# Expert blocks of two sizes, and 8 KB reads and 4 KB writes in the last stage of a Mamba, SSD and experts kernel

## The chip, the cores and the metric

The kernel runs on one core of a Trainium2 chip, in one launch. The metric is the device time of that launch in microseconds. Engines are named as in the profile: PE (matmuls; PEld its weight loads), DVE (vector), ACT (scalar), POOL (GpSimd) and SP, which here only issues DMAs.

## The reference

The input x has 4 images of 256 channels and 64 x 64 points, so 16,384 tokens of 256 channels, all in float32. Layer 0 is a gated Mamba block, layer 1 a Mamba-2 (SSD) block. After them comes a mixture of eight experts, which sends each token to the one expert with the largest gate value. Each expert takes at most 2,560 tokens (1.25 x 16384 / 8). The part that matters here, shortened:

```python
idx = jnp.argmax(probs, axis=-1)                    # one expert for a token
pos = (jnp.cumsum(one_hot, axis=0) * one_hot).sum(-1).astype(jnp.int32) - 1
buf = jnp.zeros((E, C, D), dtype=h.dtype).at[idx, pos_safe].set(x, mode='drop')
hmid = jax.nn.relu(jnp.einsum('ecd,edf->ecf', buf, w1) + b1[:, None, :])
ybuf = jnp.einsum('ecf,efd->ecd', hmid, w2) + b2[:, None, :]
y_tok = ybuf[idx, pos_g] * (prb * kept)[:, None]
```

Here E = 8, C = 2560, D = 256 and F = 1024. At the end the tokens (token by channel) are turned back into images (channel by point).

## The kernel before, in words

The program has three phases, called one after the other at the end of `tile_conv_attn_hybrid`: `mixers`, `experts` and `turn`.

**mixers** computes both layers in 64 chunks of 256 tokens. Its instructions are not issued as written: they are collected in a `Plan`, which orders them by a simulated schedule with costs and due slots, and `issue` emits them in that order (so nearly all of them have line 373 in the profile). For each token it writes the layer's output to `tok_d` in DRAM, and scatters a row of 260 numbers (probability, scale, shift, token number, 256 channels) to `buf_d`, at the slot that the token has in its expert's part of 2,560 slots.

The end of `mixers`, from line 1270, makes the tables that the experts read. `total` holds each expert's number of tokens. A block is 256 slots of one expert. From the counts the code works out how many blocks each expert needs (`blocks`), the running sum of them (`ends`), and for each of 71 blocks which expert it belongs to (`which`) and where its rows begin (`base`). The results are `row_at` (two columns of row numbers for each block) and `w_at` (the rows of the expert's weights). 71 is NT // st + NE - 1, with st = 256: enough for any routing. All 71 blocks are always run; a block without tokens reads row numbers that are out of use. The table's operations are small ones on DVE, each needing the one before it. They work in the space of three tiles of the `mid` ring, handed out by `line`.

**experts** runs over the 71 blocks. `begin(i)` (line 1351) gathers the block's rows (`rows`, two indirect DMAs of 128 rows, on POOL) and the weights of its expert (`w`, one indirect DMA of 128 x 17,440 bytes), normalises the tokens on ACT (`tn`, line 1362), converts the token numbers on DVE (`number`, line 1364) and turns the tokens on PE (`pt`, line 1369), which DVE copies to `xt` (line 1370). Then, for eight slices `f` of the hidden layer, PE computes `ph` (line 1387) with the weights as the stationary operand and the 256 tokens as the moving one; ACT makes `hid` of six slices (line 1389) and DVE of two (line 1391). In the middle of these slices `begin(i + 1)` is called. Then PE computes `po` (line 1398) for each half of 128 tokens, with `hid` as the stationary operand and 256 columns of `w2` as the moving one. DVE and ACT make the result `fixed` from it (lines 1399 to 1408), and POOL scatters it to `tok_d` with one indirect DMA for each half (line 1410). There are three buffers for `w`, four for `rows` and `number`, two for the other work tiles, and in PSUM four for `ph` and two each for `pt` and `po`. In this phase the framework's own scheduler orders the instructions of each engine when the program is built; an engine then runs them in that fixed order.

**turn** reads `tok_d` in 32 pieces of 512 tokens (`outrows`, issued by SP, line 1429), so that partition p has tokens p, p + 128, p + 256 and p + 384: pieces of 1 KB. PE turns them into `pto` (line 1434), DVE and ACT copy a channel half each to `o` (lines 1436 and 1438), and ACT issues the write (line 1439): 2 KB for a channel. There are six buffers for `outrows`, `o` and `pto`.

Of the kernel before, what the change touches and what calls it, by code (L numbers as in the profile page):

```python
# [20 lines left out]
P = 128  # L21
# [362 lines left out]
def tile_conv_attn_hybrid(ctx: ExitStack, tc: tile.TileContext, a: dict, out: bass.AP, cap: int, st: int):  # L384
# [12 lines left out]
    def nm(s):  # L397
        return f"{s}_{next(names)}"
# [9 lines left out]
    ident = const.tile([P, P], F32, name="ident")  # L408
    make_identity(nc, ident)

    nj = st // P
    nblk = NT // st + NE - 1
    row_at = const.tile([P, nblk, nj], U32, name="row_at")
    w_at = const.tile([P, nblk], U32, name="w_at")

    def column(value):
        t = const.tile([P, 1], F32, name=nm("col"), tag=nm("col"))
# [8 lines left out]
    def mixers(es):  # L426
# [214 lines left out]
        for t in (s_in, s_out, s_cb, s_cbbc, s_dtb, neg_a1, g_b, taps_x, diag_bc, diag_d1):  # L641
            t.root.lasting = True

        routed, rows_at, ws_at = r.fixed(buf_d), r.fixed(row_at), r.fixed(w_at)

        def load_x(k_, tag):
            xin = work([P, KC, T], tag)
# [639 lines left out]
        def iota(t, step, n, cm=0):  # L1287
            r.gps("iota", t, [[step, n]], 0, cm, allow_small_or_imprecise_dtypes=True)
            return t
# [2 lines left out]

            return t[:, :, None].to_broadcast([P, *n]) if inner else t[:, None].to_broadcast([P, *n])

        per = cap // st
        steps, block, which_e = iota(line(0, per), st, per), iota(line(0, nblk), 1, nblk), iota(line(0, NE), 1, NE)
        place = iota(line(0, nj), P, nj, 1)
        counts, one, blocks, ends, starts = (line(0, NE) for _ in range(5))
        which, count, base, limit = (line(0, nblk) for _ in range(4))
        some = line(0, NE, per)  # L1300
        r.gps("memset", one, 1.0)
        r.copy(counts, total)
        r.tt(some, over(counts, (NE, per), True), over(steps, (NE, per), False), ALU.is_gt)
        r.dve("tensor_reduce", blocks, some, AX.X, ALU.add)
        r.dve("tensor_tensor_scan", ends, one, blocks, 0.0, ALU.mult, ALU.add)
        r.tt(starts, ends, blocks, ALU.subtract)
        n = (nblk, NE)
        table = line(1, *n)
        r.tt(table, over(block, n, True), over(ends, n, False), ALU.is_ge)
        r.dve("tensor_reduce", which, table, AX.X, ALU.add)  # L1310
        mine = line(2, *n)
        r.tt(mine, over(which, n, True), over(which_e, n, False), ALU.is_equal)
        for sums, values in ((base, starts), (count, counts)):
            r.tt(table, mine, over(values, n, False), ALU.mult)
            r.dve("tensor_reduce", sums, table, AX.X, ALU.add)

        r.tt(base, block, base, ALU.subtract)
        r.dve("tensor_scalar", base, base, float(st), None, ALU.mult)
        r.dve("scalar_tensor_tensor", count, count, float(cap), base, ALU.min, ALU.subtract)
        r.dve("scalar_tensor_tensor", base, which, float(cap), base, ALU.mult, ALU.add)  # L1320
        r.dve("tensor_scalar", base, base, float(NSLOT), None, ALU.subtract)
        n = (nblk, nj)
        row, valid = line(2, *n), line(2, *n)
        r.tt(valid, over(count, n, True), over(place, n, False), ALU.is_gt)
        r.tt(row, over(base, n, True), over(place, n, False), ALU.add)
        r.tt(row, row, valid, ALU.mult)
        r.dve("tensor_scalar", rows_at, row, float(NSLOT), None, ALU.add)
        r.dve("tensor_scalar", which, which, float(NE - 1), float(P), ALU.min, ALU.mult)
        r.tt(ws_at, which, place[:, :1].to_broadcast([P, nblk]), ALU.add)
        r.issue()  # L1330

    def experts(es):
# [17 lines left out]

        W1, W2 = KC * FF, KF * C

        def begin(i):

            w = wp.tile([P, W1 + W2 + KF + C], F32, name=nm("w"), tag="w")
            rows = wk.tile([P, nj, ROW], F32, name=nm("rows"), tag="rows", bufs=4)
            for j in range(nj):
                gather(rows[:, j], buf_d, row_at[:, i, j : j + 1], NSLOT + P)
            gather(w, a["w_exp"], w_at[:, i : i + 1], NE * P)
            tn = wk.tile([P, nj, C], F32, name=nm("tn"), tag="tn")  # L1360
            for j in range(nj):
                act(tn[:, j], rows[:, j, TOK:], AF.Identity, scale=rows[:, j, 1:2], bias=rows[:, j, 2:3])  # L1362
            number = wk.tile([P, nj], U32, name=nm("number"), tag="number", bufs=4)
            nc.vector.tensor_copy(number, rows[:, :, 3])  # L1364
            xt = wk.tile([P, KC, st], F32, name=nm("xt"), tag="xt")
            pt = pt_p.tile([P, KC, st], F32, name=nm("pt"), tag="pt")
            for k in range(KC):
                for j in range(nj):
                    nc.tensor.transpose(pt[:, k, j * P : (j + 1) * P], tn[:, j, k * P : (k + 1) * P], ident)
            nc.vector.tensor_copy(xt, pt)  # L1370
            return w, rows, number, xt

        now = begin(0)
        for i in range(nblk):
            w, rows, number, xt = now
            w1 = w[:, :W1].rearrange("p (k f) -> p k f", k=KC)
            w2 = w[:, W1 : W1 + W2].rearrange("p (k d) -> p k d", k=KF)
            b1 = w[:, W1 + W2 : W1 + W2 + KF]
            b2 = w[:, W1 + W2 + KF :]
            hid = wk.tile([P, KF, st], F32, name=nm("hid"), tag="hid")  # L1380
            for f in range(KF):
                if f == KF // 2 and i + 1 < nblk:

                    now = begin(i + 1)
                ph = ph_p.tile([P, st], F32, name=nm("ph"), tag="ph")
                for k in range(KC):
                    mm(ph, w1[:, k, f * P : (f + 1) * P], xt[:, k], start=k == 0, stop=k == KC - 1)  # L1387
                if f % 4 != 3:
                    act(hid[:, f], ph, AF.Relu, bias=b1[:, f : f + 1])  # L1389
                else:  # L1390
                    ts(hid[:, f], ph, b1[:, f : f + 1], 0.0, ALU.add, ALU.max)
            y = wk.tile([P, nj, C], F32, name=nm("y"), tag="y")
            fixed = wk.tile([P, nj, C], F32, name=nm("fixed"), tag="fixed")
            ok = wk.tile([P, nj, C], U32, name=nm("ok"), tag="ok", bufs=1)
            po = po_p.tile([P, nj, C], F32, name=nm("po"), tag="po")
            for j in range(nj):
                for f in range(KF):
                    mm(po[:, j], hid[:, f, j * P : (j + 1) * P], w2[:, f], start=f == 0, stop=f == KF - 1)  # L1398
            tt(y, po, b2[:, None].to_broadcast([P, nj, C]), ALU.add)
            for j in range(nj):  # L1400
                act(y[:, j], y[:, j], AF.Copy, scale=rows[:, j, 0:1])

            ts(fixed, y, -1e4, 1e4, ALU.max, ALU.min)
            ts(ok, y, 0.0, 0.0, ALU.mult, ALU.is_equal)
            nc.vector.copy_predicated(fixed, ok, y)
            tt(ok, y, y, ALU.not_equal)
            nc.vector.copy_predicated(fixed, ok, zero[:, None].to_broadcast([P, nj, C]))
            tt(fixed, fixed, rows[:, :, TOK:], ALU.add)  # L1408
            for j in range(nj):
                nc.gpsimd.indirect_dma_start(  # L1410
                    out=tok_d,
                    out_offset=bass.IndirectOffsetOnAxis(ap=number[:, j : j + 1], axis=0),
                    in_=fixed[:, j],
                    in_offset=None,
                    bounds_check=NT - 1,
                    oob_is_err=False,
                )

    def turn(es):

        wk = es.enter_context(tc.tile_pool(name="out_work", bufs=6))
        pt_p = es.enter_context(tc.tile_pool(name="out_ps", bufs=6, space=PSUM))
        W = 512
        nj = W // P
        for b in range(NB):
            for c in range(L // W):
                i = b * L + c * W
                rows = wk.tile([P, nj, C], F32, name=nm("outrows"), tag="outrows")
                nc.sync.dma_start(rows, tok_d[i : i + W].rearrange("(j p) d -> p j d", p=P))  # L1429
                o = wk.tile([P, KC, W], F32, name=nm("o"), tag="o")  # L1430
                for k in range(KC):
                    pt = pt_p.tile([P, W], F32, name=nm("pto"), tag="pto")
                    for j in range(nj):
                        nc.tensor.transpose(pt[:, j * P : (j + 1) * P], rows[:, j, k * P : (k + 1) * P], ident)  # L1434
                    if k % 2 == 0:
                        nc.vector.tensor_copy(o[:, k], pt)  # L1436
                    else:
                        nc.scalar.copy(o[:, k], pt)  # L1438
                nc.scalar.dma_start(out[b].rearrange("(k p) l -> p k l", p=P)[:, :, c * W : (c + 1) * W], o)  # L1439

    for phase in (mixers, experts, turn):
# [101 lines left out]
```

## Time and profile before

| what | us |
|---|---|
| time, median of 3 runs | 6741.11 (6736.48 to 6754.15) |
| the profiled execution's own time | 6746.82 |
| its span, first to last instruction | 6745.1 |
| granted clock of PE, mean over the span | 0.957 of full |
| mixers, until the counts are copied | to 5603.0 |
| table on DVE | 5603.2 to 5611.5 |
| first `ph` matmul, end of the last `po` | 5624.0, 6643.2 |
| first read of the last stage | 6653.7 |

The profile's page gives each engine's busy time, then the span in 40 equal slices (a digit is the busy share in tenths), then DMA queues, then groups of instructions. In a group or a timeline row, `ph<-xt,w` names what is written and what is read, `x16` is the number of instructions, and the part in square brackets is how long the engine had been idle before and what ended this. In a group's line the busy time in us and the mean of one in ns follow the bar, then the idle time before the group's instructions. A float32 matmul appears as two passes. Times in a timeline count from the start of the span.

### The profile page before, as it was taken

Reading aid. Unit: us, or ns where it says so; the run is one execution under the profiler, and the core shown is the slowest. Engines: PE = TensorE matmul, PEld = TensorE weight load, DVE = VectorE, ACT = ScalarE, POOL = GpSimd, SP = SyncE. Lnnn points to the kernel's source line nnn. Section 1 sums busy time; section 2 is a strip of 40 time slices with the busy share of each in tenths; the row PEclk is TensorE's granted clock in tenths of the full one; section 3 lists DMA queues with packets and bytes.
Section 4 is the critical chain, followed back from the end, with each engine's and each line's share of the span. In section 5 each row is a group of like instructions: output and inputs, shape, how many; then the busy total and the mean of one; then the engine's idle time right before and its main releaser. Section 6 shows DMA issues by size and latency. Waiting matters only on the chain. (4 is left out here: it accounts for less than half of the span.)

```text
span 6745.1 us, 111880 instructions
## 1 busy us (share of the span) xinstructions
PE 6239.9 (93%) x37672; PEld 4330.6 (64%) x37672; DVE 5559.2 (82%) x7646; ACT 4878.5 (72%) x12007; POOL 3305.5 (49%) x2632
## 2 busy tenths in 40 slices
PE   7899999999999999999999999999999978999996
PEld 5566666666666666666666666666666546888886
DVE  5999999999999999999999999999999973344443
ACT  6888888888878888888888888888888852333332
POOL 4655555555555555555555555555555542333331
PEclk8999999999999999999999999999999988999998
DMA  6855555555555555555555555555555534555556
GB/s 189 233 151 149 151 149 151 149 147 151 152 148 153 149 148 152 152 153 152 149 150 151 151 153 147 156 151 151 153 149 150 148 92 158 186 196 190 193 191 243
DMA packets 943874, 1077.19 MB, mean 160 GB/s; under 512 B 94480, under 2 KB 912404, under 8 KB 934082
## 3 DMA queue, kind: packets, MB, share of 16 engines
q1 hardware_dynamic: 904594, 842.28, 45.0%
q0 software_dynamic: 30000, 210.98, 8.7%
q10 hardware_dynamic: 8704, 16.78, 0.6%
q8 instruction: 297, 4.87, 0.3%
q14 instruction: 279, 2.29, 0.1%
HBM read 785.70 MB, written 277.68 MB: 158 GB/s over the span
## 5 line engine op out<-in xcount | busy, mean ns | idle before, releaser
L373 POOL TENSOR_TENSOR p<-h,bc 128x1024 f32<-128x1024 f32 x1024 | 2413.7, 2357 | 1996.7 <-DVE ub L373 501.3
L373 DVE TENSOR_TENSOR_SCAN h<-da,ub 128x1024 f32<-128x1024 f32 x1024 | 2339.1, 2284 | 77.0 <-ACT da L373 4.4
L373 ACT ACTIVATE da<-dt,w_m_Alog 128x255 f32<-128x255 f32 x4096 | 1842.7, 502 | 0.0
L373 DVE TENSOR_TENSOR ub<-u,bc 128x1024 f32<-128x1024 f32 x1024 | 1279.1, 1249 | 13.9 <-DMA u<-u_d 6.5
L373 PE MATMUL py<-p,sum 128*32 128x256 f32 x8192 | 658.9, 394 | 175.1 <-POOL p L373 168.8
L373 PE MATMUL b<-t,w_W_in 128*128 128x256 f32 x2304 | 579.0, 392 | 25.2 <-ACT bcs L373 4.8
L373 PEld LDWEIGHTS b<-t,w_W_in 128*128 128x128 f32 x2304 | 418.4, 190 | 188.7 <-ACT raw L373 75.3
L1387 PE MATMUL ph<-xt,w 128*128 128x256 f32 x2272 | 516.3, 381 | 4.0 <-ACT hid L1389 3.9
L373 PE MATMUL a<-t,w_m_in_w 128*128 128x256 f32 x2048 | 513.4, 395 | 3.0 <-DVE t L373 2.7
L1398 PE MATMUL po<-w,hid 128*128 128x256 f32 x2272 | 502.0, 379 | 0.0
L373 PEld LDWEIGHTS py<-p,sum 128*32 128x32 f32 x8192 | 169.0, 108 | 497.3 <-POOL p L373 246.5
L373 PE MATMUL a<-raw,taps_m 128*128 128x256 f32 x2048 | 482.0, 383 | 4.9 <-ACT pre L373 4.9
L1398 PEld LDWEIGHTS po<-w,hid 128*128 128x128 f32 x2272 | 431.7, 190 | 58.7
L1387 PEld LDWEIGHTS ph<-xt,w 128*128 128x128 f32 x2272 | 427.0, 191 | 62.2 <-ACT hid L1389 5.7
L373 PEld LDWEIGHTS a<-t,w_m_in_w 128*128 128x128 f32 x2048 | 372.8, 191 | 145.6 <-issue 72.5
L373 PEld LDWEIGHTS a<-raw,taps_m 128*128 128x128 f32 x2048 | 378.2, 190 | 130.4 <-ACT e L373 39.8
L373 ACT COPY hlast<-h 128x4 f32<-128x4 f32 x1024 | 202.9, 198 | 273.6 <-DVE h L373 260.9
L1364 DVE CAST number<-rows 128x2 uint32<-128x2 f32 x71 | 12.0, 169 | 467.0 <-DMA tok_d<-fixed,number 455.5
L1362 ACT ACTIVATE tn<-rows 128x256 f32<-128x256 f32 x142 | 82.3, 597 | 402.9 <-DMA rows<-buf_d,row_at 397.2
L373 PE MATMUL c<-cum,after 128*128 128x512 f32 x512 | 323.8, 719 | 15.9 <-ACT dend L373 13.5
L1410 POOL DMA_INDIRECT tok_d<-fixed,number x142 | 146.1, 1029 | 391.2 <-DVE fixed L1408 308.5
L373 ACT ACT_TABLE_LOAD x256 | 328.4, 1283 | 4.5
(237 smaller groups left out, 11320.5 us busy)
## 6 DMA issues: line engine op xcount, KB each, us to landing
dt<-dt_d SPq DMA_DIRECT2D x1024, 128.0 KB, 2.8
u<-u_d SPq DMA_DIRECT2D x1024, 128.0 KB, 2.2
raw<-raw_d SPq DMA_DIRECT2D x1024, 128.0 KB, 3.6
gx_d<-pre SPq DMA_DIRECT2D x64, 1024.0 KB, 5.5
bc<-bc_d SPq DMA_DIRECT2D x1024, 64.0 KB, 2.4
gx<-gx_d SPq DMA_DIRECT2D x256, 256.0 KB, 4.8
raw_d<-raw SPq DMA_DIRECT2D x64, 518.0 KB, 3.6
dt_d<-mid SPq DMA_DIRECT2D x64, 512.0 KB
```

The lines of the kernel that those rows point to most:

```text
L373: op.issued = f(*map(placed, args), **{k: placed(v) for k, v in kw.items()})
L1362: act(tn[:, j], rows[:, j, TOK:], AF.Identity, scale=rows[:, j, 1:2], bias=rows[:, j, 2:3])
L1364: nc.vector.tensor_copy(number, rows[:, :, 3])
L1387: mm(ph, w1[:, k, f * P : (f + 1) * P], xt[:, k], start=k == 0, stop=k == KC - 1)
L1398: mm(po[:, j], hid[:, f, j * P : (j + 1) * P], w2[:, f], start=f == 0, stop=f == KF - 1)
L1410: nc.gpsimd.indirect_dma_start(out=tok_d, out_offset=bass.IndirectOffsetOnAxis(ap=number[:, j : j + 1], axis=0), in_=fixed[:, j], in_offse ...
```

## The change

Three things change, and nothing else does.

1. **Blocks of two sizes.** With 128 rows as a unit, 16384 / 128 + 7 = 135 units are enough for any routing. They become 63 blocks of 256 rows and 9 of 128, and each size has tables of its own. The code gives each expert as many big blocks as it has full use for (`pairs`: a second unit must hold tokens), in order of the experts, until 63 are given (`taken`); what is left of each expert (`rest`) goes to small blocks, which begin behind its big ones (`gone`). `line_up` spreads the small blocks evenly among the big ones.
2. **Tables.** What was done once for 71 blocks is done twice, for 63 and for 9, with a few operations ahead of it.
3. **The last stage** takes 1,024 tokens in a piece: partition p reads tokens 8p to 8p + 7, 8 KB in one run. The turned tokens are put in their order by the copy from PSUM, which writes a number to every eighth place (32 bytes apart). A write has 4 KB for a channel. DVE copies one half of the tokens in each partition, ACT the other. There are four buffers in place of six for `outrows` and `o`.

The diff, cut to its core:

```diff
-    nblk = NT // st + NE - 1
-    row_at = const.tile([P, nblk, nj], U32, name="row_at")
-    w_at = const.tile([P, nblk], U32, name="w_at")
+    units = NT // P + NE - 1
+    n_big = (units - NE) // 2
+    sizes = (nj, n_big), (1, units - nj * n_big)
+    tables = [
+        (const.tile([P, n, k], U32, name=f"row_at{k}"), const.tile([P, n], U32, name=f"w_at{k}")) for k, n in sizes
+    ]
...
+        for sums, first, step, n in ((n_units, 0, P, per), (pairs, P, 2 * P, per // 2)):
+            steps, some = line(0, n), line(0, NE, n)
+            r.gps("iota", steps, [[step, n]], first, 0, allow_small_or_imprecise_dtypes=True)
+            r.tt(some, over(counts, (NE, n), True), over(steps, (NE, n), False), ALU.is_gt)
+            r.dve("tensor_reduce", sums, some, AX.X, ALU.add)
+
+        def upto_here(ends, starts, n):
+            r.dve("tensor_tensor_scan", ends, one, n, 0.0, ALU.mult, ALU.add)
+            r.tt(starts, ends, n, ALU.subtract)
+
+        upto_here(ends, starts, pairs)
+        r.dve("tensor_scalar", taken, starts, -1.0, float(n_big), ALU.mult, ALU.add)
+        r.dve("scalar_tensor_tensor", taken, taken, 0.0, pairs, ALU.max, ALU.min)
+        r.dve("scalar_tensor_tensor", rest, taken, -2.0, n_units, ALU.mult, ALU.add)
+        r.dve("tensor_scalar", gone, taken, float(st), None, ALU.mult)
+        for (k, nblk), (rows_at, ws_at), n_blocks, behind in zip(sizes, tables, (taken, rest), (zero_e, gone)):
+            rows_at, ws_at = r.fixed(rows_at), r.fixed(ws_at)
+            upto_here(ends, starts, n_blocks)
+            r.dve("scalar_tensor_tensor", starts, starts, float(-k * P), behind, ALU.mult, ALU.add)
...
-        def begin(i):
+        def begin(nj, i):
             w = wp.tile([P, W1 + W2 + KF + C], F32, name=nm("w"), tag="w")
-            rows = wk.tile([P, nj, ROW], F32, name=nm("rows"), tag="rows", bufs=4)
+            row_at, w_at = tables[nj == 1]
+            st = nj * P
+            rows = wk.tile([P, 2, ROW], F32, name=nm("rows"), tag="rows", bufs=4)[:, :nj]
...
-        now = begin(0)
-        for i in range(nblk):
+        line_up = sorted(((i + 0.5) / n, k, i) for k, n in sizes for i in range(n))
+        now = begin(*line_up[0][1:])
+        for at, (_, nj, _) in enumerate(line_up):
+            st = nj * P
...
-        wk = es.enter_context(tc.tile_pool(name="out_work", bufs=6))
+        wk = es.enter_context(tc.tile_pool(name="out_work", bufs=4))
...
-        W = 512
+        W = 1024
         nj = W // P
+        half = nj // 2
...
-                nc.sync.dma_start(rows, tok_d[i : i + W].rearrange("(j p) d -> p j d", p=P))
+                nc.sync.dma_start(rows, tok_d[i : i + W].rearrange("(p j) d -> p j d", p=P))
                 o = wk.tile([P, KC, W], F32, name=nm("o"), tag="o")
                 for k in range(KC):
-                    pt = pt_p.tile([P, W], F32, name=nm("pto"), tag="pto")
-                    for j in range(nj):
-                        nc.tensor.transpose(pt[:, j * P : (j + 1) * P], rows[:, j, k * P : (k + 1) * P], ident)
-                    if k % 2 == 0:
-                        nc.vector.tensor_copy(o[:, k], pt)
-                    else:
-                        nc.scalar.copy(o[:, k], pt)
+                    for h in range(2):
+                        pt = pt_p.tile([P, half, P], F32, name=nm("pto"), tag="pto")
+                        for j in range(half):
+                            nc.tensor.transpose(pt[:, j], rows[:, h * half + j, k * P : (k + 1) * P], ident)
+                        to = o[:, k].rearrange("c (p j) -> c j p", j=nj)[:, h * half : (h + 1) * half]
+                        if h % 2 == 0:
+                            nc.vector.tensor_copy(to, pt)
+                        else:
+                            nc.scalar.copy(to, pt)
```

What follows in the table's loop is the old text with the block's size k * P in place of st. In the block loop of `experts`, every tile keeps the size for 256 rows and is used in part by a small block.

More of the change, by code (lines that the diff above doesn't have):

```diff
@@ L642, in mixers @@
             t.root.lasting = True
-        routed, rows_at, ws_at = r.fixed(buf_d), r.fixed(row_at), r.fixed(w_at)
+        routed = r.fixed(buf_d)
         def load_x(k_, tag):
@@ L1293, in over @@
             return t[:, :, None].to_broadcast([P, *n]) if inner else t[:, None].to_broadcast([P, *n])
[L1295 to L1300, printed above, removed]
+        per = cap // P
+        which_e, place = iota(line(0, NE), 1, NE), iota(line(0, nj), P, nj, 1)
@@ L1301, in mixers @@
+        counts, one, zero_e, n_units, pairs, ends, starts, taken, rest, gone = (line(0, NE) for _ in range(10))
         r.gps("memset", one, 1.0)
+        r.gps("memset", zero_e, 0.0)
         r.copy(counts, total)
[L1303 to L1329, printed above, removed]
+        for sums, first, step, n in ((n_units, 0, P, per), (pairs, P, 2 * P, per // 2)):
[3 more added lines that the diff above has]
+            r.dve("tensor_reduce", sums, some, AX.X, ALU.add)
@@ new lines, in mixers @@
+        for (k, nblk), (rows_at, ws_at), n_blocks, behind in zip(sizes, tables, (taken, rest), (zero_e, gone)):
+            rows_at, ws_at = r.fixed(rows_at), r.fixed(ws_at)
+            upto_here(ends, starts, n_blocks)
+            r.dve("scalar_tensor_tensor", starts, starts, float(-k * P), behind, ALU.mult, ALU.add)
+            block = iota(line(0, nblk), 1, nblk)
+            which, count, base = (line(0, nblk) for _ in range(3))
+            n = (nblk, NE)
+            table, mine = line(1, *n), line(2, *n)
+            r.tt(table, over(block, n, True), over(ends, n, False), ALU.is_ge)
+            r.dve("tensor_reduce", which, table, AX.X, ALU.add)
+            r.tt(mine, over(which, n, True), over(which_e, n, False), ALU.is_equal)
+            for sums, values in ((base, starts), (count, counts)):
+                r.tt(table, mine, over(values, n, False), ALU.mult)
+                r.dve("tensor_reduce", sums, table, AX.X, ALU.add)
+            r.dve("scalar_tensor_tensor", base, block, float(k * P), base, ALU.mult, ALU.add)
+            r.dve("scalar_tensor_tensor", count, count, float(cap), base, ALU.min, ALU.subtract)
+            r.dve("scalar_tensor_tensor", base, which, float(cap), base, ALU.mult, ALU.add)
+            r.dve("tensor_scalar", base, base, float(NSLOT), None, ALU.subtract)
+            n = (nblk, k)
+            row, valid = line(2, *n), line(2, *n)
+            r.tt(valid, over(count, n, True), over(place[:, :k], n, False), ALU.is_gt)
+            r.tt(row, over(base, n, True), over(place[:, :k], n, False), ALU.add)
+            r.tt(row, row, valid, ALU.mult)
+            r.dve("tensor_scalar", rows_at, row, float(NSLOT), None, ALU.add)
+            r.dve("tensor_scalar", which, which, float(NE - 1), float(P), ALU.min, ALU.mult)
+            r.tt(ws_at, which, place[:, :1].to_broadcast([P, nblk]), ALU.add)
@@ L1359, in begin @@
             gather(w, a["w_exp"], w_at[:, i : i + 1], NE * P)
-            tn = wk.tile([P, nj, C], F32, name=nm("tn"), tag="tn")
+            tn = wk.tile([P, 2, C], F32, name=nm("tn"), tag="tn")
             for j in range(nj):
                 act(tn[:, j], rows[:, j, TOK:], AF.Identity, scale=rows[:, j, 1:2], bias=rows[:, j, 2:3])
-            number = wk.tile([P, nj], U32, name=nm("number"), tag="number", bufs=4)
+            number = wk.tile([P, 2], U32, name=nm("number"), tag="number", bufs=4)[:, :nj]
             nc.vector.tensor_copy(number, rows[:, :, 3])
-            xt = wk.tile([P, KC, st], F32, name=nm("xt"), tag="xt")
-            pt = pt_p.tile([P, KC, st], F32, name=nm("pt"), tag="pt")
+            xt = wk.tile([P, KC, 2 * P], F32, name=nm("xt"), tag="xt")[:, :, :st]
+            pt = pt_p.tile([P, KC, 2 * P], F32, name=nm("pt"), tag="pt")[:, :, :st]
             for k in range(KC):
@@ L1379, in experts @@
             b2 = w[:, W1 + W2 + KF :]
-            hid = wk.tile([P, KF, st], F32, name=nm("hid"), tag="hid")
+            hid = wk.tile([P, KF, 2 * P], F32, name=nm("hid"), tag="hid")[:, :, :st]
             for f in range(KF):
-                if f == KF // 2 and i + 1 < nblk:
-                    now = begin(i + 1)
-                ph = ph_p.tile([P, st], F32, name=nm("ph"), tag="ph")
+                if f == KF // 2 and at + 1 < len(line_up):
+                    now = begin(*line_up[at + 1][1:])
+                ph = ph_p.tile([P, 2 * P], F32, name=nm("ph"), tag="ph")[:, :st]
                 for k in range(KC):
@@ L1391, in experts @@
                     ts(hid[:, f], ph, b1[:, f : f + 1], 0.0, ALU.add, ALU.max)
[L1392 to L1395, printed above, removed]
+            y = wk.tile([P, 2, C], F32, name=nm("y"), tag="y")[:, :nj]
+            fixed = wk.tile([P, 2, C], F32, name=nm("fixed"), tag="fixed")[:, :nj]
+            ok = wk.tile([P, 2, C], U32, name=nm("ok"), tag="ok", bufs=1)[:, :nj]
+            po = po_p.tile([P, 2, C], F32, name=nm("po"), tag="po")[:, :nj]
             for j in range(nj):
```

## The prediction

> **What bounds the kernel now.** I read the page's busy slices first, to find the stages, then the view of stretches, the groups by shape, the timeline of two blocks and the DMA queues of the last stage.
>
> ```profile
> PE   7899999999999999999999999999999978999996
> PEclk8999999999999999999999999999999988999998
> GB/s 189 233 151 149 151 149 151 149 147 151 152 148 153 149 148 152 152 153 152 149 150 151 151 153 147 156 151 151 153 149 150 148 92 158 186 196 190 193 191 243
> ```
>
> A slice is 168.6 us. The first 33 are the mixers, which the change leaves as they are but for the table at their end; then six slices of experts with a full PE; in the last slice PE drops and the DMA rate is the highest of the run. The stretches sharpen this (columns: length; PE, PEld, DVE, ACT, POOL busy with counts; clock, DMA share, GB/s):
>
> ```profile
> 5590.00:5624.00 34.00, 11.76 (x41) 9.18 (x41) 13.59 (x49) 3.42 (x10) 11.98 (x14) 0.55 0.35 132
> 6200.00:6400.00 200.00, 198.22 (x945) 174.00 (x944) 82.72 (x154) 65.33 (x141) 72.07 (x71) 1.00 0.54 194
> 6680.00:6700.00 20.00, 13.52 (x72) 11.73 (x70) 5.53 (x8) 3.42 (x6) 0.00 (x0) 0.68 1.07 380
> ```
>
> So there are three regimes. Around 5603 to 5624 nearly everything waits for the table and the first gather. The experts (5624 to 6643) are bound by PE at full clock, with DMA half used. The last stage (6654 to 6745) is bound by the DMA engines: share 1.07 (records overlap a little), PE and copies waiting.
>
> **The pace of the experts.** Groups by shape, then one block in the timeline:
>
> ```profile
> L1387 PE MATMUL ph<-xt,w 128*128 128x256 f32 x2272 | 516.3, 381 | 4.0 <-ACT hid L1389 3.9
> L1398 PE MATMUL po<-w,hid 128*128 128x256 f32 x2272 | 502.0, 379 | 0.0
> ```
>
> ```profile
> 6106.45 7.07 PE L1398 MATMUL po<-w,hid 128*128 128x256 f32 x32
> 6107.51 1.03 POOL L1410 DMA_INDIRECT tok_d<-fixed,number  x1 [4.22 <-DVE fixed L1408]
> ...
> 6113.36 3.62 PE L1387 MATMUL ph<-xt,w 128*128 128x256 f32 x16
> 6115.17 0.17 DVE L1364 CAST number<-rows 128x2 uint32<-128x2 f32 x1 [7.55 <-DMA tok_d<-fixed,number]
> 6115.25 0.68 DVE L1399 TENSOR_TENSOR y<-po,w 128x512 f32<-128x512 f32 x1
> 6116.03 0.91 ACT L1401 ACTIVATE y<-y,rows 128x256 f32<-128x256 f32 x2 [2.33 <-DVE y L1399]
> ...
> 6116.84 1.18 ACT L1389 ACTIVATE hid<-ph,w 128x256 f32<-128x256 f32 x3
> ```
>
> 2272 is 71 x 32: the program has 16 matmuls of each kind in a block, and each appears as two passes. Passes of 256 columns start 0.216 us apart in the instruction records, so a block takes 64 x 0.2158 + 4 transposes x 0.109 = 14.25 us. The po groups start from 5632.85 to 6636.16: 1003.3 / 70 = 14.33 us a block, so waits cost only 0.08. But the rows in between show a second loop of nearly the same length: scatter, its landing, number, y, and so to the next scatter. From one y to the next (6100.80 to 6115.25) it took 14.45 us. Here y starts about 2 us after its po has ended, and ACT's first hid comes behind it.
>
> **Part 1: 63 blocks of 256 and 9 of 128.** 135 units of 128 rows come from 16384/128 + 7; n_big = (135 - 8) // 2 = 63, and 9 are left. All blocks run whatever the routing. Eight big blocks go, 9 small ones come, one after about every seven big. A small block has 32 passes of ph with 128 columns, 16 of po with 256 (half the tokens) and 2 transposes. The nearest row for a 128-column pass is this one, eight passes loading weights as ph does:
>
> ```profile
> 5583.63 0.97 PEld L373 LDWEIGHTS c<-pre,diag_d 128*128 128x128 f32 x8 [0.44 <-ACT bt L373]
> ```
>
> (0.97 - 0.19) / 7 = 0.111, and the instruction records of that group have 0.111 or 0.112 in 750 of 896 pairs. So 32 x 0.1115 + 16 x 0.2157 + 2 x 0.109 = 7.24 us, half of a big one. Without waits: 63 x 14.33 + 9 x 7.24 = 968.0 against 71 x 14.33 = 1017.4, or -49.4.
>
> What lies beside a small block doesn't halve: it still finishes the big block before it. DVE must do y 0.69, fixed 0.43, ok 0.63, copies 0.75 and 0.73, compare 0.69, add 0.68 of that block, the next xt 0.68, number 0.17, and two hid of half size (0.35 each, an estimate from 0.48): 6.15 us, plus about 1.0 of waiting for ACT's y (73.6 us in 71 waits): 7.2 of 7.24 us. ACT's hid slices may stand behind y; with four ph buffers PE's fifth slice, about 1.9 us into a small block, needs hid 0, where in the rows above ACT got to hid 3.5 us after po's end. The wait is bounded by 0 (the order issued puts hid ahead of y) and about 3 us (fifth slice and xt both late). The nearest row, PEld waiting for ACT hid, has 5.7 us in 8 waits, 0.7 each; I take 1.0 a small block, as DVE has no slack there: 9 us. Experts: -49.4 + 9 = -40.
>
> Weights: one more gather of 2.23 MB, but DMA has half its time free, and three buffers leave 7.2 + 14.3 = 21.5 us from a gather to its use across a small block; 128 packets of 17,440 B at a median 649 ns over 16 engines take 5.2 us. Nothing. The seven fewer row gathers and scatters on POOL are under PE's cover: also nothing.
>
> **Part 2: tables.** This chain is bare: PE idles until the first rows land. Before, DVE needs 8.3 us from the counts (5603.21) to row_at (5611.50). After, priced by the same rows (0.20 from start to start of a tiny operation, 0.28 at 80 elements, 0.78 at 568): a head of ten operations 2.5, the 63-block table 8.0 (504 elements at 0.70 seven times), the 9-block table 4.3 (72 elements at 0.24). The gather of block 0 needs only the first table, so the lower bound is 10.5 - 8.3 = +2; as the planner fills DVE's gaps with the second, the upper is 14.8 - 8.3 = +6.5. I take +4. The extra iotas and memsets on POOL depend on nothing and run earlier.
>
> **Part 3: the last stage.** Its queues:
>
> ```profile
> q1 hardware_dynamic: 16896, 16.78, 53.9%
> q10 hardware_dynamic: 8704, 16.78, 47.3%
> ```
>
> These are 16384 reads of 1 KB and 8192 writes of 2 KB (the rest are 4-byte signals), together 101% of the engines. The packet records by size have medians of 46 ns for 1,024 B, 84 for 2,048, 159 for 4,096 and 309 for 8,192 (the load of w_m_in_w), on one line: 8.5 ns a packet and 37.6 a KB. After, reads are 2048 of 8 KB and writes 4096 of 4 KB: (2048 x 309 + 4096 x 159) / 16 = 80.3 us, against (16384 x 46 + 8192 x 84) / 16 = 90.1: -9.8. [...] The last piece is 512 KB longer, at 400 GB/s 1.3 us at the tail: -8.5.
>
> [...] The new copies write 4 bytes every 32. No row of this trace has such a write of any size[...]; contiguous, the copies take 0.69 (DVE) and 0.59 (ACT), 32 on each engine. By the row they are 22 us beside 80 of DMA; doubled (my value) 44, still hidden; they decide from 80/32 = 2.5 us, 3.6 times the row. Below zero I exclude: they do the same work.
>
> **Sum.** -40 + 4 - 8.5 = -44.5. The profiled execution took 6746.8 (span 6745.1), 5.7 above the median; I take the difference off the median: 6741.1 - 44.5 = 6696.6, rounded to 6697.
>
> **Rivals.**
> - PE waits 3 us in each small block (DVE and ACT full, as above): 9 x 2 more, 6715. For it: 7.2 of 7.24 us. Against it: a big block after each small one gives slack back.
> - The strided copies bound the last stage, at 2.9 us each: 32 x 2.9 + 3 at the ends = 96 against 91.4; +4.6 in place of -8.5, so 6710. [...]
> - No waits, table at its lower bound: -49.4 + 2 - 9.8, 6684.
> - Slower: number stands ahead of y on DVE in the small blocks too and waits for a landing that comes no sooner. y to y stays 14.4 us, so y is 7 us late; hid of the block behind waits and PE stops about 6.5 us, at two numbers 13. Then a small block costs 20.3 us: +68 + 4 - 8.5, 6805. It decides from (1017.4 + 4.5 - 902.8) / 9 = 13.2 us. For it: number waits 455.5 us in 67 waits; against it: that wait falls in idle DVE time, and a small block's own chain has one scatter, not two.
> - That the blocks aren't fewer can't be: their numbers are fixed when built.
>
> **Chances.** Forecast 0.63; long waits 0.20 (0.03 of it within 0.3%); copies 0.08 (0.02 of it); no waits 0.06; slower 0.03. A measurement can tell about 0.3%, 20 us. Faster 0.92, same 0.05, slower 0.03. The range runs from the no-wait case to just past the long waits: 6682 to 6720.
>
> **What would show it.** Right: 2016 ph passes of 256 columns and 288 of 128, the small ones about 0.112 apart; small blocks of 7.3 to 9 us; PE's waits for hid or xt near 9 us; the first ph about 4 us later; last stage near 83 us at over 400 GB/s; its copies under 2.5 us. Wrong: number or y late across small blocks, or last-stage PE waiting for DVE's o while the DMA share falls under 0.9.

## The result, and the profile after

| | before | after |
|---|---|---|
| time, median, us | 6742.75 (6736.48 to 6754.15, 4 runs) | 6705.86 (6699.94 to 6709.76, 4 runs) |
| ratio, 95% interval | | 0.9943 [0.9925, 0.996] |
| profiled execution, its span, us | 6746.8, 6745.1 | 6706.9, 6704.9 |

The medians are 36.9 us apart, the profiled spans 40.2. Predicted were 44.5. By stage, from the two profiles:

| stage | before | after | difference | predicted |
|---|---|---|---|---|
| mixers, until the counts are copied | 5603.0 | 5602.7 | -0.4 | 0 |
| counts to the first `ph` | 21.0 | 22.4 | +1.5 | +4 |
| experts, first `ph` to the start of the last `po` pass | 1018.9 | 982.6 | -36.2 | -40 |
| last `po` pass to the first read of the last stage | 10.9 | 11.2 | +0.3 | 0 |
| last stage | 91.4 | 86.0 | -5.4 | -8.5 |

So nearly nine tenths of the gain lie in the experts, as forecast, and in this pair of profiles all three terms that were forecast came out smaller. One caution for small terms: the mixers have the same code in all kernels here, and ended anywhere from 5577 to 5615 us in their profiles. A few microseconds of a total can't be given to a stage; what follows therefore compares stages, and repeats where a kernel has a stage unchanged. Nine profiles have the changed kernel's experts: 974.5 to 984.7, mean 979.2. Three have its last stage: 84.5 to 86.0, mean 85.1; three have the old one: 91.1 to 91.4. In twelve profiles of kernels with two sizes of block, the first `ph` comes 1.0 to 1.5 us later after the counts than before the change. By these means the experts gain 39.7 us (against the one profile of the kernel before) and the last stage 6.2.

The busy slices of the changed kernel, to be laid beside those shown above (a slice is now 167.6 us):

```profile
PE   7899999999999999999999999999999977999997
PEclk8999999999999999999999999999999988999998
GB/s 188 234 149 150 150 147 151 146 151 152 152 153 152 149 145 151 146 150 150 152 148 150 153 153 153 153 153 152 151 153 152 149 102 143 199 199 195 200 197 260
```

The picture is the same: mixers, a gap around the tables, experts with a full PE, a last stage with the highest rate. Groups by shape, in the experts alone:

```profile
L1422 PE MATMUL po<-w,hid 128*128 128x256 f32 x2160 | 478.0, 379 | 0.0
L1411 PE MATMUL ph<-xt,w 128*128 128x256 f32 x2016 | 458.8, 381 | 6.4 <-ACT hid L1413 6.2
L1411 PE MATMUL ph<-xt,w 128*128 128x128 f32 x288 | 37.3, 278 | 5.8 <-ACT hid L1413 5.7
```

There are 2016 = 63 x 32 passes of `ph` with 256 columns, 288 = 9 x 32 with 128, and 112 fewer of `po`: the work that was predicted. What is new stands behind the last bar: PE's idle time ahead of `ph` was 4.0 us before and is 12.2 now, nearly all of it for ACT's `hid`, and nearly half of it in the nine small blocks. The last stage, before (first fence) and after (second), in the stretches view with the columns as above (length; busy time and count of PE, PEld, DVE, ACT, POOL; clock; DMA share; GB/s):

```profile
6664.00:6734.00 70.00, 40.85 (x207) 34.42 (x206) 17.39 (x26) 14.34 (x26) 0.00 (x0) 0.68 1.07 389
```

```profile
6637.00:6697.00 60.00, 37.15 (x192) 30.61 (x192) 24.03 (x24) 25.16 (x24) 0.00 (x0) 0.72 1.02 423
```

The rate in the middle rose from 389 to 423 GB/s. DVE and ACT do more (24 of 60 us, where it was 17 and 14 of 70), and are far from full.

### The profile page after: what moved, and what is told of

Same layout as the page of the kernel before. It is cut to its first block, busy times and chain, and to the rows that moved or that the text cites. A ratio compares the mean times of both kernels' runs of the same rounds, so it can differ in the third digit from the quotient of the medians.

```text
span 6704.9 us, 111610 instructions
## 1 busy us (share of the span) xinstructions
PE 6188.0 (92%) x37578; PEld 4282.6 (64%) x37578; DVE 5552.4 (83%) x7685; ACT 4879.5 (73%) x11999; POOL 3295.2 (49%) x2622
## 5 line engine op out<-in xcount | busy, mean ns | idle before, releaser
L1411 PE MATMUL ph<-xt,w 128*128 128x256 f32 (+1 forms) x2304 | 496.1, 368 | 12.2 <-ACT hid L1413 11.9
L1422 PE MATMUL po<-w,hid 128*128 128x256 f32 x2160 | 478.0, 379 | 0.0
L1411 PEld LDWEIGHTS ph<-xt,w 128*128 128x128 f32 x2304 | 412.3, 190 | 69.5 <-ACT hid L1413 17.9
L1422 PEld LDWEIGHTS po<-w,hid 128*128 128x128 f32 x2160 | 409.7, 190 | 55.3
L1385 DVE CAST number<-rows 128x2 uint32<-128x2 f32 x72 | 12.3, 170 | 450.1 <-DMA tok_d<-fixed,number 437.7
```

## The experiments

**The experts.** Theory 1: the waits in the small blocks come from the token numbers. `number` has four buffers; a scatter holds its buffer until its rows have landed (`number` waits for that 68 times in the changed kernel, 437.7 us in all); so DVE, which has `number` ahead of `y`, stops, and ACT's `y` and `hid` come late behind it. The rival is the prediction's reason: DVE has no slack in a small block. The timeline of one small block of the changed kernel (the fourth):

```profile
6105.46 1.95 PE L1411 MATMUL ph<-xt,w 128*128 128x128 f32 x16
6106.17 0.37 ACT L1413 ACTIVATE hid<-ph,w 128x128 f32<-128x128 f32 x1 [0.55 <-PE ph L1411]
6106.94 0.17 DVE L1385 CAST number<-rows 128x2 uint32<-128x2 f32 x1 [7.61 <-DMA tok_d<-fixed,number]
6107.02 0.68 DVE L1423 TENSOR_TENSOR y<-po,w 128x512 f32<-128x512 f32 x1
...
6107.74 0.91 ACT L1425 ACTIVATE y<-y,rows 128x256 f32<-128x256 f32 x2 [1.20 <-DVE y L1423]
...
6108.55 0.86 ACT L1413 ACTIVATE hid<-ph,w 128x128 f32<-128x128 f32 x3
...
6108.95 1.27 PE L1411 MATMUL ph<-xt,w 128*128 128x128 f32 x9 [0.66 <-ACT hid L1413]
```

The fourth row is `y` of the block whose `po` ended at 6105.46. It starts 1.56 us late, and the row above it says why: DVE had been idle for 7.61 us, for a scatter's landing. ACT makes its first `hid`, then waits for `y` (1.20); three `hid` stand behind, and PE has no free `ph` for 0.66 us.

*e1, eight buffers for the numbers.*

```diff
-            number = wk.tile([P, 2], U32, name=nm("number"), tag="number", bufs=4)[:, :nj]
+            number = wk.tile([P, 2], U32, name=nm("number"), tag="number", bufs=8)[:, :nj]
```

> The changed kernel with eight buffers for number in place of four, so that number no longer waits for the landing of a scatter, only for its rows. Theory 1 (the waits in small blocks come from y starting late, because number stands ahead of it on DVE and waits for a landing): y starts within 0.3 us of the end of its po, the small blocks fall from a mean of 8.37 us to 7.3 to 7.6, the one of 11.28 us is gone, the big ones fall from 14.41 to about 14.3, and the experts get 10 to 16 us shorter. Theory 2 (DVE and ACT are simply full during a small block, with 6.15 us of work in 7.24): the small blocks stay at 8 us or more and the stage within 3 us of what it was.

Measured: 6688.82 (6675.33 to 6692.55), ratio 0.9926 [0.991, 0.9943]; experts 965.0, which is 14.2 below the mean of 979.2. The same small block with eight buffers:

```profile
6085.56 1.95 PE L1411 MATMUL ph<-xt,w 128*128 128x128 f32 x16
6085.76 0.69 DVE L1423 TENSOR_TENSOR y<-po,w 128x512 f32<-128x512 f32 x1 [1.35 <-PE po L1422]
6086.26 0.37 ACT L1413 ACTIVATE hid<-ph,w 128x128 f32<-128x128 f32 x1 [1.49 <-PE ph L1411]
...
6087.78 1.95 PE L1411 MATMUL ph<-xt,w 128*128 128x128 f32 x16
```

`y` starts 0.20 us after `po`, and PE runs its two times sixteen passes without a wait. The waits of the experts (us in total, times, longest), first of the changed kernel and then of e1:

```profile
DVE number L1385 <- DMA tok_d<-fixed,number: 437.7, 68, 10.6
...
PE ph L1411 <- ACT hid L1413: 11.9, 19, 2.4
```

```profile
DVE number L1385 <- DMA rows<-buf_d,row_at: 299.1, 70, 7.8
...
PE ph L1411 <- ACT hid L1413: 0.6, 2, 0.3
```

`number` still waits, but now for its own rows, which come in time; PE's wait is gone. DVE has the same operations in both kernels, so a DVE without slack was not the cause: eight of nine small blocks run at 7.46 us, their pace without any wait. One thing came along with the buffers: once behind each small block the scheduler moved a `number` from behind two `hid` and an `xt` to ahead of them. Everywhere else, in the block shown too, DVE keeps its order.

*e9, five buffers* (the same line, `bufs=5`).

> The changed kernel with five buffers for number in place of four. Four buffers make the number of a block wait for the scatter of the block four back; its rows, with four buffers of their own, wait only for the add that comes before that scatter. So one buffer more should be as good as four more: small blocks at 7.46 us but for the third, big ones at 14.25, the experts 965 us within 2. If it is the distance to the landing that counts, more than one buffer is needed and the stage stays above 970.

Measured, in one run: 6691.91 beside 6733.13 of the kernel before; experts 963.9. One buffer more does all of it (with the same order on DVE as in e1).

*e5, the kernel before with eight buffers* (the same edit in the old text).

> The kernel before (71 blocks of 256, old last stage) with eight buffers for number. If the wait of number delays y there as well, but a big block hides it, then y's mean delay after its po falls from 0.85 us to about 0.2, the blocks fall from 14.36 to 14.25 to 14.28 and the experts from 1018.9 to 1012 to 1014: 5 to 7 us, less than half of the 17.6 that the same edit takes off the kernel with small blocks. If the small blocks had nothing to do with it, it takes off as much here as there.

Measured: 6742.12 beside 6751.85, ratio 0.9984 [0.9976, 0.9993]; experts 1012.8, or 6.1 less than before. Here DVE, ACT and POOL keep the order that they had, so that the buffers alone took the wait away. It was there before the change too, and was worth 6 us; the change raised it to 14. With it gone from both, the two sizes of block gain 1012.8 - 965.0 = 47.8 us, where the sum without waits gave 49.4.

One small block stands out: the third took 11.3 us in the changed kernel, 12.5 to 14.2 in others. POOL's timeline there (first fence), and at the same place in the kernel before (second):

```profile
5876.77 1.03 POOL L1361 DMA_INDIRECT w<-in_w_exp_dram,w_at  x1 [5.76 <-DVE ok L1430]
5878.94 1.03 POOL L1434 DMA_INDIRECT tok_d<-fixed,number  x1 [1.14 <-DVE fixed L1432]
...
5887.07 1.02 POOL L1434 DMA_INDIRECT tok_d<-fixed,number  x1 [4.46 <-DMA tok_d<-fixed,number]
```

```profile
5873.82 1.03 POOL L1342 DMA_INDIRECT w<-in_w_exp_dram,w_at  x1 [5.86 <-ACT hid L1389]
5876.25 1.03 POOL L1410 DMA_INDIRECT tok_d<-fixed,number  x1 [1.39 <-DVE fixed L1408]
```

The weights' gather of 2.23 MB always stands ahead of a scatter in POOL's order; here it came late. POOL stood idle for 5.76 us before it, where 3.1 is the median, and the scatter followed after 2.2 us. That scatter, which `number` waits for, landed late: the next one was let go 8.1 us after it. The kernel before has the same late gather (5.86 us) and lost 2.1 us in the block there (16.32 us against 14.25). So the small blocks did not bring it; they made it dearer. With five or eight buffers this block took 8.1 to 8.8 us. That the weights' transfer is what held up the scatter is read from the order of the rows, not tested, and why the gather came late is open.

**The last stage.**

*e2, the old last stage with the new blocks* (`turn` as before the change).

> The changed kernel with the last stage as it was (512 tokens, 1 KB reads, 2 KB writes, six buffers): the blocks and tables alone. If the parts add up, the stages up to the first read of the last stage stay as in the changed kernel (6619 us) and the last stage takes 91.4 us again, 5.4 more than the 86.0 of the changed kernel; the time is then about 31 us below the kernel before. If the parts act on each other (the last stage's larger tiles moving the experts' buffers or order), the experts differ by more than 3 us.

Measured: 6700.21 (6693.04 to 6720.98), ratio 0.9945 [0.9926, 0.9964]; experts 976.0, last stage 91.1. The stages add up: the old code takes its old 91 us. The total doesn't show the 5 us; in its profile the mixers ended 8.6 us earlier and the experts took 6.6 less.

*e4, reads of 1 KB and writes of 4 KB.*

```diff
-                nc.sync.dma_start(rows, tok_d[i : i + W].rearrange("(p j) d -> p j d", p=P))
+                nc.sync.dma_start(rows, tok_d[i : i + W].rearrange("(j p) d -> p j d", p=P))
...
-                        to = o[:, k].rearrange("c (p j) -> c j p", j=nj)[:, h * half : (h + 1) * half]
+                        to = o[:, k].rearrange("c (j p) -> c j p", j=nj)[:, h * half : (h + 1) * half]
```

> The changed kernel, but a partition reads tokens p, p + 128 and so on, in pieces of 1 KB, and the copies from PSUM are contiguous; pieces of 1,024 tokens, four buffers and 4 KB writes stay. The law of 8.5 ns a packet and 37.6 a KB: (16384 x 46 + 4096 x 159) / 16 = 87.8 in place of 80.3, so the last stage takes 7.5 us more than 86.0, about 93.5, and more than before, and the copies take 0.69 and 0.59 us again. If the strided copies were what holds the stage, it gets shorter or stays at 86 although the reads are small.

Measured: 6703.26 (6690.91 to 6705.9), ratio 0.994 [0.9922, 0.9958]; last stage 91.1. The middle of that stage:

```profile
6630.00:6694.00 64.00, 31.91 (x191) 28.16 (x189) 16.59 (x24) 13.80 (x24) 0.00 (x0) 0.73 1.06 390
```

The 4 KB writes, without the longer reads, brought nothing: 390 GB/s against 389. So the gain needs the longer reads.

*e11, long reads and contiguous copies* (only the second line of e4's edit; the tokens are then not put in their order).

> The changed kernel with contiguous copies from PSUM while a partition still reads eight neighbouring tokens: it leaves out the putting of a piece's tokens in their order, so the output's points are permuted within 1,024. It shows what the step of 32 bytes costs alone. If the strided copies are hidden, the copies take 0.69 and 0.59 us and the last stage still 84.5 to 86.0. If they hold part of it, it takes under 83.5.

Measured, in one run: 6688.66 beside 6733.13; last stage 84.7. Its copies, then those of the changed kernel, as groups of the last stage:

```profile
L1464 DVE COPY o<-pto 128x512 f32<-128x512 f32 x32 | 21.2, 689 | 60.1 <-DMA out_dram<-o 41.3 <-PE pto L1461 18.7
L1466 ACT COPY o<-pto 128x512 f32<-128x512 f32 x32 | 18.6, 586 | 67.0 <-DMA out_dram<-o 34.6 <-PE pto L1461 32.3
```

```profile
L1466 ACT COPY o<-pto 128x512 f32<-128x512 f32 x32 | 33.8, 1098 | 53.9 <-PE pto L1461 29.6 <-DMA out_dram<-o 24.2
L1464 DVE COPY o<-pto 128x512 f32<-128x512 f32 x32 | 32.2, 1084 | 50.9 <-DMA out_dram<-o 32.3 <-PE pto L1461 18.6
```

Writing every eighth number made DVE's copy 1.57 times as long (689 to 1084 ns) and ACT's 1.87 times (586 to 1098). The stage is 84.7 with the short copies and 84.5 to 86.0 with the long ones: they are hidden.

*e8, each copy twice* (both `tensor_copy(to, pt)` and `copy(to, pt)` issued two times).

> The changed kernel with each copy from PSUM to o issued twice (the second writes the same numbers to the same place), so 2.2 us of DVE and of ACT in place of 1.1, 70 us of each in the last stage. If the strided copies are hidden behind the DMA, the stage takes at most 2.5 us more than 84.5 to 86 (the first and the last piece show the longer copies). If they are part of what holds it, it takes 92 us or more.

Measured: 6710.48 (6690.44 to 6712.11), ratio 0.9941 [0.9923, 0.996]; last stage 93.5. Its middle:

```profile
6613.00:6673.00 60.00, 35.52 (x184) 29.14 (x183) 47.73 (x47) 43.87 (x46) 0.00 (x0) 0.73 0.99 405
```

With 2.2 us of copies for each `pto` tile the copies decided here, although DVE is busy for only 47.7 of 60 us: PE waits for DVE's `o` 16 times, and the pieces come every 5.4 us where the changed kernel's come every 5.0.

*e3, six buffers in the last stage* (`out_work`, `bufs=4` to `bufs=6`).

> The changed kernel with six buffers of 1,024 tokens in the last stage in place of four. Theory A (the missing 3 us are lost at the start: the four read buffers are full before the first piece has been turned, so the DMA engines have little to do at about 8 us, at 189 GB/s): with six buffers the dip is gone or shorter, the stage takes 83 to 84.5 us. Theory B (the loss is the strided copies, 1.1 us each in place of 0.69 and 0.59, or the long tail): the stage stays at 86 within 0.5.

Measured: 6695.62 (6691.35 to 6700.83), ratio 0.9935 [0.9918, 0.9951]; last stage 84.9, inside the 84.5 to 86.0 of four buffers. The dip of the DMA rate at the start is shallower (335 GB/s in its lowest slice, 221 in the changed kernel), but it is 333 in e1 with four buffers too: a gain is not shown.

*e7, pieces of 512 tokens* (`W = 512`, eight buffers: reads of 4 KB, writes of 2 KB, copies of half the width).

> The changed kernel with pieces of 512 tokens in the last stage, eight buffers: 4 KB reads, 2 KB writes, copies that write to every fourth place (16 bytes apart). If the size of the reads makes the gain and that of the writes none, it is about as quick as with 8 KB and 4 KB, 84 to 86 us, since shorter pieces also shorten the two ends. By the law of 8.5 ns a packet it would take 3.4 us more in the middle: 87 to 89. The copies take 1.1 us as before if any step of 16 bytes or more costs the same, 0.7 if 16 is still free.

Measured: 6720.67 (6715.21 to 6727.63), ratio 0.996 [0.9945, 0.9974]; last stage 103.7, a clear miss. PE waits for DVE's `o` 48 times, 24.1 us in all, and DVE and ACT wait for PE. The DMA engines are full from 20 to 50 us after the first read (a busy share of 0.9 or more in every slice, 415 GB/s), while the reads run ahead, and over half idle in the last 26 us (166 GB/s). Two readings offered themselves: two half tiles in one PSUM bank (a bank is here the space of one tile of 128 x 512) get in each other's way, or the many short copies, each handing over to PE, are what costs.

*e10, one whole-bank tile for each channel half:*

```diff
-                    for h in range(2):
-                        pt = pt_p.tile([P, half, P], F32, name=nm("pto"), tag="pto")
...
+                    pt = pt_p.tile([P, nj, P], F32, name=nm("pto"), tag="pto")
...
+                    to = o[:, k].rearrange("c (p j) -> c j p", j=nj)
```

> As with pieces of 512 tokens before, but one PSUM tile of a whole bank for each channel half, DVE copying one and ACT the other as in the kernel before (steps of 16 bytes). If the 103.7 us came from two half-bank tiles in one bank, between whose transposes and copies PE waited (24.1 us for DVE's o), PE no longer waits so and the stage takes 84 to 87 us: 4 KB reads and 2 KB writes by the packet law, less the overlap seen so far. If reads of 4 KB are themselves slow, it stays above 90.

Measured, in one run: 6707.84 beside 6733.13; last stage 87.0, 413 GB/s in the middle, PE's wait for DVE's `o` 16.0 us. I took this for the bank, but the copies had also become half as many and twice as wide. So:

*e12, e7 with a bank of its own for each half tile* (`pt_p.tile([P, nj, P], ...)[:, :half]`).

> The kernel with pieces of 512 tokens whose last stage took 103.7 us, with one change: each half-bank pto tile (128 x 256) gets a PSUM bank of its own, and only half of the bank is used. Instructions, their sizes and their number stay the same. Bank theory: PE waited for DVE because two half tiles, one copied by DVE and one by ACT or written by PE, lay in one bank; then the last stage falls to 85 to 89 us, as with one whole-bank tile per channel half (87.0), and PE's wait for DVE's o falls from 24.1 us to 16 or less. Size theory: twice as many copies of half the width, each with its own handshake with PE, are what costs; then the last stage stays at 100 us or more.

Measured, in one run: 6717.82 beside 6746.37; last stage 103.2, and PE's wait for DVE's `o` is what it was in e7 (us, times, longest):

```profile
PE pto L1461 <- DVE o L1464: 24.1, 48, 0.8
```

The bank reading falls. The size of the hand-overs alone isn't the answer either, by e12's own trace. In its steady part a piece comes every 3.26 us, and PE stands still twice in it behind a copy of DVE's, for 0.75 and 0.28 us. But the first seven pieces, with the same copies and the same hand-overs, took 12 us, or 1.7 us each (14 copies of each engine in the first stretch). What differs is PE's clock (first stretch: the first pieces; second: the steady part):

```profile
6617.00:6629.00 12.00, 9.19 (x60) 7.52 (x59) 7.78 (x14) 8.15 (x14) 0.00 (x0) 0.89 1.00 374
6640.00:6670.00 30.00, 20.70 (x74) 13.09 (x74) 10.92 (x18) 11.43 (x19) 0.00 (x0) 0.50 1.04 414
```

In the first stretch PE was busy for 0.15 us a transpose (9.19 us for 60), in the second for 0.28 (20.70 for 74). So the slow pace goes with a PE at half its clock, 0.50 where it was 0.89. What lowers the clock, whether the short copies keep it there, and why PE waits for so recent a copy with six buffers, is open.

**Together.** *e6, eight buffers for the numbers and six in the last stage.*

> Eight buffers for number and six of 1,024 tokens in the last stage, the version that the first runs point to. The experts as with eight alone (965 us), the last stage 84 to 85 us, so 52 to 58 us below the kernel before.

Measured: 6688.64 (6681.21 to 6693.67) beside 6751.85, ratio 0.9914 [0.989, 0.9938]; experts 965.5, last stage 84.7. The ratio is below the changed kernel's 0.9943, but the two were not measured side by side and their intervals overlap. In the stages it is the experts that are 14 us shorter, and e1 (6688.82) has this by the number buffers alone.

## Why the prediction was right, point by point

- **The sum.** -44.5 predicted, -40.2 between the profiles and -36.9 between the medians. 6705.9 lies in the range, 9 us above the forecast. What was to bring the gain did bring it: fewer passes on PE, and longer reads. How well the terms fit is less certain. By the means of the repeats the experts gained 39.7 where 40 was put, the last stage 6.2 where 8.5 was put, and the tables cost 1.0 to 1.5 where 4 was put. The last two errors are in opposite directions and nearly cancel, which is luck.
- **The pace of a small block, 7.24 us.** Right, though not to be read off one block: without waits a small block takes 7.46, as it also turns the next, big block (four transposes), and the big block ahead of it 14.03, as it turns a small one. Their sum, 21.49, is the 14.25 + 7.24 of the forecast.
- **Waits of 1.0 us a small block.** Right in size: 8.37 - 7.46 = 0.91. The reason given, DVE with 7.2 of 7.24 us to do, was wrong: e1 leaves DVE its work and takes the waits. So the 9 us were right by luck. The mechanism is that of the slower rival, `number` ahead of `y`, but at 0.9 us a small block where that rival put 13. It had `y` 7 us late; in the small block shown it was 1.56 us late. What was said against it, that the wait falls in idle time of DVE, did not hold even before the change: there it cost 6 us (e5).
- **"Weights: ... Nothing."** This failed in one place: around the late gather the third small block took 3.8 us too long, nearly half of the 8.2 us of all nine (the rest is 0.55 each). The same late gather cost 2.1 us in the kernel before, so at most the difference comes from the change.
- **The big blocks.** Put at their old pace. Their waits rose from 7.8 us in all to 12.1, about 4 us, and e1 and e9 take most of these away too (1 to 1.5 us are left). With 8.2 in the small blocks this brings -49.4 to -37, beside -36.2 in the same profile.
- **Tables, +4.** Mis-sized: +1.5, which is below the lower bound of +2. I priced the second table by whole operations in gaps; in fact the planner interleaved the two chains, and their tiny operations start 0.13 to 0.2 us apart. The timeline of the changed kernel:

```profile
5602.65 0.17 ACT L373 COPY mid<-c 128x8 f32<-128x8 f32 x1 [1.27 <-PE c L373]
...
5612.22 0.23 DVE L373 TENSOR_SCALAR row_at<-mid 128x126 uint32<-128x126 f32 x1
...
5613.38 0.37 DVE L373 TENSOR_SCALAR row_at<-mid 128x9 uint32<-128x9 f32 x1
5613.94 0.27 DVE L1358 MEMSET zero<- 128x256 f32 x1 [0.18 <-DVE row_at L373]
5614.61 1.01 POOL L1361 DMA_INDIRECT rows<-buf_d,row_at  x1 [0.83 <-DVE zero L1358]
```

  From the counts to `row_at` of the big blocks DVE took 9.6 us where it took 8.3. By the profile the first row gather waits for a memset (`zero`) that stands behind the second table on DVE, so both tables count; it comes 1.7 us later after the counts than before.
- **Last stage, -8.5.** The direction and the engine that decides were right, the size was not: -5.4, or -6.2 by the means. Of 33.55 MB, 389 GB/s makes 86.3 us and 423 makes 79.3: -7.0, where the packet law said -9.8. Its packets were right: in the changed kernel's last stage the median of 8 KB is 309 ns and that of 4 KB 159. But the law added up packets' times as if no two lay beside each other. That they did was to be seen: a share of 1.07 before and 1.02 after. Divided by these, the law's own 90.1 and 80.3 become 84.2 and 78.7, or -5.5. What lies around the middle grew from 5.1 to 6.7 us, about as put (+1.3).
- **Strided copies.** Put at 1.4 us, twice the contiguous copy, which was my estimate as no row of before has such a write, and hidden; 1.08 and 1.10, and hidden (e11). The 2.9 us of the rival that they bound the stage had no measurement behind it. The point from which they decide was put at 2.5 us and is lower: 2.2 us already decide (e8), which I read as the hand-overs between PE and the copies, that the division by 32 left out; no run tests this. Against contiguous copies they are 1.57 and 1.87 times as long (e11), where the estimate was twice.

## What to carry to other kernels

When steps become smaller, look at what each step holds until a transfer has landed, not only at how busy the engines are: here one more buffer of a tile of 8 bytes a partition took 14 us off the experts, where the new block sizes took 48 (with that buffer in both kernels). Before adding up the times of packets, look whether their records overlap: here the share of the DMA engines was 1.07 before and 1.02 after, and a gain of 9.8 by the sum came out as 7.0. And when an experiment changes two things, as e10 did, its reading is a guess until a second one (e12) holds one of them still. Nor does the fall of one reading prove the other: look for a place in the same trace where the one that is left should hold too.

## What was not expected of the hardware

- The size of writes to DRAM made no difference beside 1 KB reads (389 GB/s with 2 KB, 390 with 4 KB); reads of 4 and 8 KB made 413 (with 2 KB writes, e10) and 423.
- Writing every fourth number cost as much as writing every eighth: 1.06 and 1.09 us for DVE and ACT in e10, 1.08 and 1.10 in the changed kernel, for tiles of 128 x 512.
- In e7 and e12 PE's granted clock is 0.53 in the middle of the last stage (stretches view), against 0.74 in e10, with the same number of transposes in all. In e12 it was 0.89 while the first pieces went through, at 1.7 us each where the later ones took 3.26.
